# Two attention-style layers on one core: value products of two token chunks issued as one group, and more unit products in the first waits

## The chip, the cores and the metric

The kernel runs on one NeuronCore of a Trainium2 chip, in one launch. The metric is device time in microseconds (us) of a whole execution. The core has a tensor engine (TensorE, PE in the profile, its weight loads PEld), a vector engine (VectorE, DVE), a scalar engine (ScalarE, ACT), a general engine (GpSimd, POOL) and a queue engine that here only issues DMAs (SyncE, SP). Each engine works through its own instructions in order, and waits on semaphores for the others.

## The reference

Eight sequences of 512 tokens, 512 features, pass through two layers, all in float32. Layer 0 is linear attention with 8 heads; layer 1 is softmax attention with 16 heads of 32. Around each stands a layer norm, projections, a second norm with a scale and shift computed from a condition vector, a SiLU, an output projection and a residual. The change touches layer 1's middle:

```python
xn = layer_norm(x, norm_w, norm_b)
q = (xn @ q_w + q_b).reshape(Bx, Tx, H, -1)
k = (xn @ k_w + k_b).reshape(Bx, Tx, H, -1)
att = jnp.einsum('bnhl,bmhl->bnmh', q, k)
att = att + (1.0 - mask) * -1000000.0
att = jax.nn.softmax(att, axis=2)
v = ((xn @ v_w + v_b) * src_mask[:, :, None]).reshape(Bx, Tx, H, -1)
y = jnp.einsum('bnmh,bmhl->bnhl', att, v).reshape(Bx, Tx, Dx)
```

## The kernel before

**How it is recorded and ordered.** The body of the kernel does not issue instructions. It calls a recorder (`Order`), which keeps each operation with the tiles it reads and writes and an assumed cost. `place` then runs a list scheduler over the record twelve times, with priorities taken from the slack of the last round, and keeps the best; `issue` writes the instructions out in the order of the planned starts. So a change in what is recorded can move any instruction of any engine. Because `issue` writes nearly everything out, nearly every row of the profile has the line L501, and rows are told apart by tiles. `order.together(cost)` records several tensor-engine calls as one operation that is not split. `order.on("gpsimd", "vector")` lets the scheduler choose the engine.

**Buffers.** Tile pools are rings with a fixed number of buffers (`BUFS`, `BANKS`): ten 128x512 buffers named A, and eight PSUM banks named mm, which scores, maxima, projections, transposes, sums and value products share. PSUM banks may be taken out of the recorded order, A buffers may not.

**Layer 1.** The work goes by heads groups G = 4 b + g: sequence b, and four heads. For one G:
- `l1_qk` projects queries and keys, splits each into a high and a low part, and writes them to DRAM; `l1_stack` reads them back as stacked operands kst and qst of 98 and 106 rows, in rings of three (G % 3).
- `l1_max` makes 16 score products (98 rows, `mm<-kst,qst` in the profile), of which VectorE takes the row maxima (nm). They are transposed (`mm<-ident,mi`), copied to z and written by a 64 KB DMA into rows 98 to 106 of qst, so that the next products come out with the maximum subtracted.
- `l1_att` makes the 16 score products again, transposed (106 rows, `mm<-qst,kst`), one for each of four token chunks m and four heads j. ScalarE takes the exponential of each into an A buffer e.
- `l1_av` makes the four value products of chunk m: v's 32 columns of each head are the weights, e is streamed, and the four products lie side by side in the array's columns and write 32 rows each of one bank (`mm<-A,v`, 128*32). They accumulate over m. It also records the running sum acc = e(0) + e(1) + e(2) + e(3), four additions for each m > 0 on POOL or VectorE.
- `l1_den` sums acc over tokens by products with a constant eg, of the same 32-column form; it is recorded in one group with the value products of chunk 0 of the next G.

`l1_att` calls `l1_av(G, m - 1)` after the second score of chunk m, and chunk 3 is called at the beginning of the next G, so there are four groups of value products for each G. The last G has a form of its own (`l1_last`), in halves of 256 columns. Two exponentials, (m, j) = (2, 2) and (2, 3), go to the spare buffers bWq and bWk instead of A (`SPARE`), since the ten A buffers hold acc and the exponentials of two chunks. Around all this run the projections of the next sequence (`ahead`) and the second half of the one before (`behind_front`), fed in by small due times.

**Unit products.** `spare` (line 476) looks for planned idle time of TensorE. Before an operation that takes a fresh tile, it counts how many products of the identity with itself fit, at 240 ns each after a margin of 1000 ns, or 480 ns each for operations planned to start before 21 us (`WARM`). `issue` writes that many such products (line 497) into the bank that the operation is about to overwrite.

Of the kernel before, what the change touches and what calls it, by code (L numbers as in the profile page):

```python
# [21 lines left out]
P = 128  # L22
NC = S // P
# [164 lines left out]
class Room:  # L188
# [19 lines left out]
    def next(self):  # L208
        if self.free and self.head in self.queue:
            return self.queue.pop(self.head)  # L210
        if self.loose and len(self.free) > 1 and self.queue:
            return self.queue.pop(min(self.queue, key=lambda i: self.queue[i].key))


class Order:
# [260 lines left out]
    def spare(self):  # L476


        fill, last = {}, None
        for o in sorted((o for o in self.ops if o.engine == "PE"), key=lambda o: o.start):  # L480
            if o.fresh:
                since = max([last.start + last.takes["PE"][1] if last else IDENT] + [t.since for t in o.fresh])
                each = SPARE_TIME * (2 if o.start < WARM else 1)
                fill[o] = int(max(0.0, o.start - WEIGHTS - MARGIN - since) / each)
            last = o
        return fill

    def issue(self, nc, unit):
        fill = self.spare()
        for p in self.pools:  # L490
            p.build()
        with self.tc.manual_schedule():
            for o in sorted(self.ops, key=lambda o: (o.start, o.seq)):
                engine = getattr(nc, o.takes[o.engine][0])
                for _ in range(fill.get(o, 0)):
                    bank = o.fresh[0].root()
                    engine.matmul(bank[:, 0:P], unit[:, 0 : bank.shape[0]], unit, start=True, stop=True)
                for method, args, kw in o.calls:
                    args = [a.real() if isinstance(a, View) else a for a in args]
                    kw = {k: v.real() if isinstance(v, View) else v for k, v in kw.items()}  # L500
                    getattr(engine, method)(*args, **kw)  # L501
# [45 lines left out]
def kernel(ctx: ExitStack, tc: tile.TileContext, x, cond, mask0, mask1, w0, w1, out):  # L547
    real, order = tc.nc, Order(tc)
    nc = order
# [14 lines left out]
    def big(tag, name, dtype=F32, shape=(P, 512)):  # L564
        t = sb.tile(list(shape), dtype, name=name, tag=tag, bufs=BUFS[tag])
        if tag == "stk":
            nc.gpsimd.memset(t[:, :, 0:1].bitcast(F32), 0.0)
        return t

    def bank(tag, name, parts=P):  # L570
        tag = {"S": "mm", "ST": "mm", "a": "mm"}.get(tag, tag)
        return ps.tile([parts, 512], F32, name=name, tag=tag, bufs=BANKS[tag])

    def mm_bank(name):
        return bank("mm", name)

    def chunk(i):
        return slice(i * P, (i + 1) * P)
# [193 lines left out]
    st = {}  # L772
# [284 lines left out]
        st["max"] = G  # L1057
        yield

    SPARE = {(2, 2): "bWq", (2, 3): "bWk"}  # L1060

    def l1_att(G):
        b, g = divmod(G, 4)
        q, k = qst[G % 3], kst[G % 3]
        if g == 0:
            st["yT", b] = []
        assert st["max"] >= G
        st["yp", G] = bank("a", f"yT{G}")
        st["acc", G] = []
        for m in range(NC):  # L1070
            cur = []
            for j in range(4):
                sp = bank("ST", f"t{G}{m}{j}")
                nc.tensor.matmul(sp, k[:, j, chunk(m)], q[:, j, :], start=True, stop=True)
                e = big(SPARE.get((m, j), "A"), f"e{G}{m}{j}")
                nc.scalar.activation(e, sp, AF.Exp)
                cur.append(e)
                if j == 1 and m > 0:
                    l1_av(G, m - 1)
                yield  # L1080
            st["e", G, m] = cur

    def l1_av(G, m):
        b, g = divmod(G, 4)
        while len(st["L1", "v", b]) <= m:
            st["need"]()
        es, yp = st.pop(("e", G, m)), st["yp", G]
        with order.together(845.0 if m or not G else 1690.0):
            if m == 0 and G > 0:
                den = l1_den(G - 1)  # L1090
            for j in range(4):
                h = 4 * g + j
                nc.tensor.matmul(
                    yp[32 * j : 32 * j + 32, :],
                    st["L1", "v", b][m][:, 32 * h : 32 * h + 32],
                    es[j],
                    start=(m == 0),
                    stop=(m == NC - 1),
                )
        if m == 0 and G > 0:  # L1100
            l1_den_keep(G - 1, den)
        acc = st["acc", G]
        if m == 0:
            acc.extend(es)
        else:
            for j in range(4):
                with order.on("gpsimd", "vector"):
                    nc.gpsimd.tensor_tensor(acc[j], acc[j], es[j], ALU.add)
        if m == NC - 1:
            t = big("yT", f"yTs{G}")  # L1110
            nc.scalar.copy(t, st.pop(("yp", G)))
            st["yT", b].append(t)
# [58 lines left out]
    def l1_den(G):  # L1171
        g = G % 4
        den = mm_bank(f"den{G}")
        acc = st.pop(("acc", G))
        for j in range(4):
            nc.tensor.matmul(den[32 * j : 32 * j + 32, :], eg[:, g, :], acc[j], start=True, stop=True)
        return den

    def l1_den_keep(G, den):
        b, g = divmod(G, 4)  # L1180
        if g == 0:
            st["dn", b] = big("dn", f"dn{b}")
# [184 lines left out]
    def ahead(b):  # L1367

        n = b + 1
        if b > 0:  # L1370
            yield from values("L1", b)
            yield from l1_qk(4 * b + 3)
        if n < B:
            if b > 0:
                while st.get(("tail", b - 1)) != NC - 1:
                    yield 0
                load_x("L1", n, x1[n])
            yield from transpose_x("L1", n)
            for g in range(3 if n else 4):
                yield from l1_qk(4 * n + g)  # L1380
# [7 lines left out]
    for b in range(B):  # L1388
        plan = []
        if b > 0:  # L1390
            plan.append([behind_front(b), 6, 34 if b < B - 1 else 70, TAIL, 0.0])
            plan.append([ahead(b), 0, 20, HEAD, 0.0])
        if b < B - 1:
            plan.append([plan[1][0] if b else ahead(b), 34 if b else 0, 64, NEXT, 0.0])

        def step(p):
            c = next(p[0], None)
            if not c:
                return False
            p[4] += c  # L1400
            return True

        def pump(i):
            go = True
            while go:
                go = False
                for p in plan:
                    due = p[3] * min(1.0, max(0.0, (i + 1 - p[1]) / (p[2] - p[1])))
                    if p[4] < due and step(p):
                        go = True  # L1410

        def need():
            for p in reversed(plan):
                if step(p):
                    return
            raise AssertionError("nothing left")

        st["need"] = need
        for g in range(4):
            G = 4 * b + g  # L1420
            if G > 0:
                l1_av(G - 1, NC - 1)
            for i, _ in enumerate(l1_att(G) if G < NG - 1 else l1_last(G)):
                next(maxes, None)
                if b == B - 1 and g == 0 and i % 4 == 0:
                    for _ in range(2):
                        next(maxes, None)
                if i == STK and 0 < G < NG - 2:
                    while ("d", "Wq", G + 2) not in st:
                        need()  # L1430
                    l1_stack(G + 2)
                pump(16 * g + i)
        if b < B - 1:
            for p in plan:
                while step(p):
                    pass
    b = B - 1
# [50 lines left out]
```

## Time and profile before

| what | value |
|---|---|
| runs shown | 1376.63, 1385.99, 1386.61 us; median 1385.99 |
| profiled execution | 1377.14 us, of which the span from first to last instruction is 1375.1 |
| mean granted TensorE clock | 0.995 |
| score products, 98 rows (`mm<-kst,qst`) | 512, 201.6 us busy |
| score products, 106 rows, 512 wide (`mm<-qst,kst`) | 496, 185.4 us |
| value products from A buffers, 512 wide (`mm<-A,v`) | 868 records, 138.8 us |
| value products from bWq and bWk | 62 records each, 32.4 us each |
| sum products, 512 wide (`mm<-A,eg`) | 248 records, 33.0 us |
| unit products (L497) | 94 records, 13.4 us |
| additions of exponentials on POOL / VectorE (`A<-A,A`) | 249 at 1358 ns / 73 at 1176 ns |
| row maxima (VectorE, `nm<-mm`) | 512 at 683 ns |

Busy time counts records, which overlap: four products that lie side by side run together, and a product's end is modelled. So the distance from one start to the next says more about TensorE than the durations do. A product in float32 of the 32-column form leaves two records. The chain of work that ended last is read in order of time; a piece "PE mm x411" is a stretch in which TensorE waited for nothing.

### The profile page before, as it was taken

The page shows a single profiled execution, that of the slowest core. Times are in us where ns is not written, and L with a number is a line of the kernel's source. Part 1 is how long each engine was busy: PE and PEld are TensorE (multiplying, and loading weights), DVE is VectorE, ACT ScalarE, POOL GpSimd, SP SyncE. Part 2 cuts the span into 40 slices and gives each one's busy share as a digit, 9 for nine tenths or more (in the row PEclk, how much of TensorE's full clock was granted, in tenths as well). Part 3 has the DMA queues.
Part 4 walks back from the last instruction along what each step waited for, and adds up shares of the span by engine and source line. Part 5 has one row for each costly group of instructions (what it writes and reads, how often), then busy time and mean ns, then how long its engine had stood idle before and what let it go on. Part 6 is the DMA issues. An engine that isn't in the chain of part 4 may idle for free.

```text
span 1375.1 us, 21070 instructions
## 1 busy us (share of the span) xinstructions
PE 1351.2 (98%) x7457; PEld 951.9 (69%) x7457; DVE 1036.2 (75%) x1771; ACT 746.6 (54%) x1400; POOL 682.3 (50%) x748
## 2 busy tenths in 40 slices
PE   7999999999999999999999999999999999999998
PEld 6788788888888887556566566566566666656655
DVE  6676676667757778887878778778878867877886
ACT  4433334443344635646746855855864764774674
POOL 6222504133242625675556548538637645664673
PEclk8999999999999999999999999999999999999999
DMA  6332202022231374553264363462553545436222
GB/s 226 133 123 100 92 10 101 17 84 86 77 100 40 131 231 122 143 150 103 86 181 107 99 186 98 125 187 64 150 155 96 146 128 135 131 100 171 65 71 72
DMA packets 77376, 158.87 MB, mean 116 GB/s; under 512 B 8556, under 2 KB 8680, under 8 KB 77248
## 3 DMA queue, kind: packets, MB, share of 16 engines
q1 hardware_dynamic: 77152, 157.41, 39.0%
q8 instruction: 59, 0.97, 0.3%
q14 instruction: 45, 0.37, 0.1%
q0 software_dynamic: 64, 0.08, 0.0%
q10 hardware_dynamic: 56, 0.04, 0.0%
HBM read 104.92 MB, written 50.48 MB: 113 GB/s over the span
## 4 chain that ended last, share of the span: by engine, by line
PE 91%; DVE 3%; ACT 3%; DMA 2%; issue 1%; SPq 0%; ACTq 0%; POOL 0%; POOLq 0%
PE mm L501 91%; ACT mm L501 1%; DVE nm L501 1%; DMA qst<-z 1%; DVE A L501 1%; ACT y L501 1%; DMA kst<-dWk 0%; DVE xc L501 0%; ACT A L501 0%; DMA rawL0Wk<-in_L_cond_Wk 0%; DMA out<-y 0%; DMA v<-in_mask_BxS_ff 0%; DVE mi L501 0%; DMA rawL0Wv<-in_L_cond_Wv 0%; ACT hhL L501 0%
## 5 line engine op out<-in xcount | busy, mean ns | idle before, releaser
L501 POOL TENSOR_TENSOR A<-A,A 128x512 f32<-128x512 f32 x249 | 332.9, 1358 | 210.9 <-PE mm L501 144.4
L501 DVE TENSOR_REDUCE nm<-mm 128x1 f32<-128x512 f32 x512 | 332.4, 683 | 69.5 <-PE mm L501 66.3
L501 ACT ACTIVATE A<-mm 128x512 f32<-128x512 f32 x450 | 250.6, 602 | 142.2 <-PE mm L501 134.8
L501 PE MATMUL mm<-kst,qst 98*128 98x512 f32 x512 | 201.6, 420 | 2.2 <-DMA out<-y 1.7
L501 PE MATMUL mm<-qst,kst 106*128 106x512 f32 (+1 forms) x528 | 192.3, 404 | 2.2 <-DMA qst<-z 1.3
L501 PEld LDWEIGHTS mm<-kst,qst 98*128 98x128 f32 x512 | 96.1, 191 | 71.8 <-issue 19.3
L501 PE MATMUL mm<-A,v 128*32 128x512 f32 (+1 forms) x932 | 143.8, 587 | 0.0
L501 PEld LDWEIGHTS mm<-qst,kst 106*128 106x128 f32 x528 | 97.3, 189 | 53.1 <-issue 14.2
L501 POOL TENSOR_TENSOR y<-y,bo 128x512 f32<-128x512 f32 x60 | 78.4, 1312 | 100.9 <-DMA y<-in_x 98.3
L501 PE MATMUL mm<-Wvh,xT 128*128 128x512 f32 x384 | 120.5, 403 | 0.0
L501 PE MATMUL mm<-xT,Wkh 128*128 128x512 f32 x384 | 117.7, 414 | 1.1 <-ACT xT L501 0.8
L501 ACT ACTIVATE mm<-mm,cols 128x512 f32<-128x512 f32 x64 | 48.2, 752 | 122.7 <-PE mm L501 122.7
L501 POOL TENSOR_SCALAR v<-bWv,cols 128x512 f32<-128x512 f32 x64 | 47.4, 753 | 114.6 <-PE mm L501 114.6
L501 ACT ACTIVATE y<-mm,shL,scL 128x128 f32<-128x128 f32 (+1 forms) x144 | 76.3, 530 | 51.1 <-PE mm L501 48.5
L501 PE MATMUL mm<-ident,xc 128*128 128x128 f32 x512 | 91.6, 282 | 10.1 <-DVE xc L501 7.2
L501 DVE TENSOR_TENSOR A<-A,A 128x512 f32<-128x512 f32 x73 | 85.2, 1176 | 13.6 <-PE mm L501 11.1
L501 PEld LDWEIGHTS mm<-ident,xc 128*128 128x128 f32 x512 | 64.4, 143 | 39.1 <-DVE xc L501 8.6
L501 PEld LDWEIGHTS mm<-xT,Wkh 128*128 128x128 f32 x384 | 70.0, 192 | 22.4 <-ACT xT L501 6.0
L501 PEld LDWEIGHTS mm<-Wvh,xT 128*128 128x128 f32 x384 | 71.9, 190 | 16.5 <-issue 1.7
L501 ACT ACTIVATE mm<-mm,shL,scL 128x128 f32<-128x128 f32 (+2 forms) x152 | 76.0, 500 | 7.2 <-PE mm L501 7.2
L501 PE MATMUL mm<-xT,Wqh 128*128 128x512 f32 x256 | 76.5, 399 | 0.3 <-DVE nm L501 0.2
L501 POOL MEMSET bWk<- 64x4 f32 (+1 forms) x24 | 5.8, 243 | 136.2 <-PE mm L501 135.4
(206 smaller groups left out, 2724.0 us busy)
## 6 DMA issues: line engine op xcount, KB each, us to landing
kst<-dWk SPq DMA_DIRECT2D x96, 256.0 KB
qst<-dWq SPq DMA_DIRECT2D x96, 256.0 KB
dWk<-hl SPq DMA_DIRECT2D x32, 512.0 KB
dWq<-hl SPq DMA_DIRECT2D x32, 512.0 KB
xc<-in_x SPq DMA_DIRECT2D x32, 256.0 KB
y<-in_x SPq DMA_DIRECT2D x32, 256.0 KB
x<-y SPq DMA_DIRECT2D x32, 256.0 KB
xc<-x SPq DMA_DIRECT2D x32, 256.0 KB
```

The lines of the kernel that those rows point to most:

```text
L501: getattr(engine, method)(*args, **kw)
```

## The change

Three things, all in recording and ordering; the arithmetic is the same.

1. `l1_av` takes a tuple of chunks. `l1_att` calls it for chunk 0 after the second score of chunk 1, and for chunks 1 and 2 together after the second score of chunk 3; chunk 3 follows at the beginning of the next G, as before. The eight value products of chunks 1 and 2 are one operation that isn't split. The value bank yp is taken from the ring when the first value products are recorded, not at the start of `l1_att`.
2. The two exponentials that use the spare buffers are those of chunk 1 (j = 2, 3), not of chunk 2.
3. Unit products are counted before any tensor operation that is a transpose or opens an accumulation, not only before one that takes a fresh tile. For operations planned before 21 us they are counted at 300 ns each after a margin of 300 ns. They are no wider than the tile that is about to be written.

```diff
-            if o.fresh:
+            method, args, kw = o.calls[0]
+            if method == "transpose" or kw["start"]:
+                each, margin = (300.0, 300.0) if o.start < WARM else (SPARE_TIME, MARGIN)
                 since = max([last.start + last.takes["PE"][1] if last else IDENT] + [t.since for t in o.fresh])
-                each = SPARE_TIME * (2 if o.start < WARM else 1)
-                fill[o] = int(max(0.0, o.start - WEIGHTS - MARGIN - since) / each)
+                fill[o] = int(max(0.0, o.start - WEIGHTS - margin - since) / each)
...
-                    bank = o.fresh[0].root()
-                    engine.matmul(bank[:, 0:P], unit[:, 0 : bank.shape[0]], unit, start=True, stop=True)
+                    to = o.calls[0][1][0].real()
+                    n = min(P, to.shape[1])
+                    engine.matmul(to[:, 0:n], unit[:, 0 : to.shape[0]], unit[:, 0:n], start=True, stop=True)
...
-    SPARE = {(2, 2): "bWq", (2, 3): "bWk"}
+    SPARE = {(1, 2): "bWq", (1, 3): "bWk"}
...
-        st["yp", G] = bank("a", f"yT{G}")
...
-                if j == 1 and m > 0:
-                    l1_av(G, m - 1)
+                if j == 1 and m in (1, 3):
+                    l1_av(G, (0,) if m == 1 else (1, 2))
...
-    def l1_av(G, m):
+    def l1_av(G, ms):
...
-        es, yp = st.pop(("e", G, m)), st["yp", G]
-        with order.together(845.0 if m or not G else 1690.0):
-            if m == 0 and G > 0:
-                den = l1_den(G - 1)
-            for j in range(4):
...
+        ess = [st.pop(("e", G, m)) for m in ms]
+        den = ms[0] == 0 and G > 0
+        with order.together(845.0 * (len(ms) + den)):
+            if den:
+                dp = l1_den(G - 1)
+            if ms[0] == 0:
+                st["yp", G] = bank("a", f"yT{G}")
+            yp = st["yp", G]
+            for m, es in zip(ms, ess):
+                for j in range(4):
...
-                l1_av(G - 1, NC - 1)
+                l1_av(G - 1, (3,))
```

More of the change, by code (lines that the diff above doesn't have):

```diff
@@ L1077, in l1_att @@
                 cur.append(e)
-                if j == 1 and m > 0:
-                    l1_av(G, m - 1)
+                if j == 1 and m in (1, 3):
+                    l1_av(G, (0,) if m == 1 else (1, 2))
                 yield
             st["e", G, m] = cur
-    def l1_av(G, m):
+    def l1_av(G, ms):
         b, g = divmod(G, 4)
-        while len(st["L1", "v", b]) <= m:
+        while len(st["L1", "v", b]) <= ms[-1]:
             st["need"]()
-        es, yp = st.pop(("e", G, m)), st["yp", G]
-        with order.together(845.0 if m or not G else 1690.0):
-            if m == 0 and G > 0:
-                den = l1_den(G - 1)
-            for j in range(4):
[L1092 to L1101, printed above, removed]
+        ess = [st.pop(("e", G, m)) for m in ms]
[8 more added lines that the diff above has]
+                for j in range(4):
+                    h = 4 * g + j
+                    nc.tensor.matmul(
+                        yp[32 * j : 32 * j + 32, :],
+                        st["L1", "v", b][m][:, 32 * h : 32 * h + 32],
+                        es[j],
+                        start=(m == 0),
+                        stop=(m == NC - 1),
+                    )
+        if den:
+            l1_den_keep(G - 1, dp)
         acc = st["acc", G]
-        if m == 0:
-            acc.extend(es)
-        else:
+        for es in ess:
+            if not acc:
+                acc.extend(es)
+                continue
             for j in range(4):
@@ L1108, in l1_av @@
                     nc.gpsimd.tensor_tensor(acc[j], acc[j], es[j], ALU.add)
-        if m == NC - 1:
+        if ms[-1] == NC - 1:
             t = big("yT", f"yTs{G}")
```

## The prediction, made before the changed kernel had run

> **What bounds the kernel now.** I read the page's busy and slice rows first, then the chain in order of time, the busy time by stage, and the TensorE timeline around the groups that the change touches.
>
> ```profile
> PE 1351.2 (98%) x7457; PEld 951.9 (69%) x7457; DVE 1036.2 (75%) x1771; ACT 746.6 (54%) x1400; POOL 682.3 (50%) x748
> PEclk8999999999999999999999999999999999999999
> PE 91%; DVE 3%; ACT 3%; DMA 2%; issue 1%; SPq 0%; ACTq 0%; POOL 0%; POOLq 0%
> ...
> 883.00:992.00 109.00, 108.31 (x551) 68.45 (x549) 85.54 (x137) 69.86 (x136) 65.13 (x62) 1.00 0.48 131
> 992.00:1101.00 109.00, 107.84 (x548) 68.37 (x549) 85.26 (x137) 69.43 (x135) 65.05 (x61) 1.00 0.47 130
> ...
> 897.86 80.33 PE mm L501 x411
> 980.46 7.36 PE mm L501 x32
> 988.45 3.72 DMA qst<-z
> 992.31 14.24 PE mm L501 x76
> ```
>
> TensorE is busy for 98% of the span and carries 91% of the chain. The windows' columns are stretch, length, busy us (count) of TensorE, its weight loads, VectorE, ScalarE and POOL, granted clock, DMA share, GB/s. In the second layer a batch takes 108.7 us (the chain's 992.31 returns at 1101.03), of which TensorE fills 108; VectorE, the next, has 85. So time can come only out of TensorE's own stream: useless intervals inside it, or waits. One wait stands on the chain in every batch, for the 64 KB write of the row maxima into the stacked operand (DMA qst<-z).
>
> The inside of the stream is seen in the timeline of TensorE (start, duration, what; one product of the 32-column kind leaves two records, so x8 is a group of four):
>
> ```profile
> 813.83 1.10 PE L501 MATMUL mm<-xT,Wql 128*128 128x512 f32 x4
> 814.86 1.06 PE L501 MATMUL mm<-A,eg 128*32 128x512 f32 x8
> 815.74 1.04 PE L501 MATMUL mm<-A,v 128*32 128x512 f32 x8
> 816.71 0.50 PE L501 MATMUL mm<-kst,qst 98*128 98x512 f32 x1
> 817.04 0.40 PE L501 MATMUL mm<-qst,kst 106*128 106x512 f32 x1
> ...
> 819.38 0.39 PE L501 MATMUL mm<-qst,kst 106*128 106x512 f32 x1
> 819.70 1.07 PE L501 MATMUL mm<-A,v 128*32 128x512 f32 x8
> 820.70 0.50 PE L501 MATMUL mm<-kst,qst 98*128 98x512 f32 x1
> 821.04 0.39 PE L501 MATMUL mm<-qst,kst 106*128 106x512 f32 x1
> ```
>
> Starts count here, since ends are modelled. Full-width products start 0.235 us apart. A lone group: from the last full start before it (819.38) to the second after it (821.04) is 1.66; less two full intervals (0.47), a group costs 1.19. A double group (sums `eg`, then values): from 813.83 + 1.10 - 0.39 = 814.54 to 817.04 is 2.50, less 0.47 is 2.03. So a group that joins another costs 0.84 to 0.86 instead of 1.19: entering and leaving the 32-column form costs 0.34. Over all groups between full-width products the medians are 1.661 (76 lone ones) and 2.517 (20 double ones): 2 x 1.661 - 2.517 - 0.466 = 0.339.
>
> **The merge.** The change issues token chunks 1 and 2 as one group. In the order that the built programs issue there are 143 unbroken runs of 32-column products before and 111 after: 31 heads groups have one run of eight value products in place of two of four, and one lone group of sums joins values. The 528 value and 132 sum products stay the same in number, and the scheduler did not break the pairs up. 32 x 0.339 = **-10.8 us**, all of it in a stream with nothing else to wait for. That two value groups in a row cost no more than sums and values in a row isn't seen in this trace (none stand together); the nearest row is the emb products of layer one, which accumulate twice into one bank with pass starts 0.41 to 0.43 us apart, as in the double group. Bounds: -8 to -11.5.
>
> **What the merge moves.** Chunk 1's exponentials wait until chunk 2's are there, so two of them move to the spare buffers bWq and bWk, which chunk 2 had. Ten A buffers and two spares are then all held (4 running sums, 8 exponentials). In the issue order a score whose exponential reuses a buffer comes within 1.5 us of the group that frees it 49 times, against 17 of 496. TensorE does not wait for the exponential itself, but for the PSUM bank behind it. Banks are taken again at the same least distance, about 1.2 us of TensorE work (48 times after, 31 before); before, those 31 waited 0.12 us in all. I take nothing for it, with 0 to 3 us as bounds. In return the value bank is taken at the first group, not at the first score, which leaves the ring of eight a bank more for some 4 us in each heads group.
>
> Seven additions of exponentials go from POOL (306 to 299) to VectorE (78 to 85): 7 x 1.176 us (the A<-A,A row) is 8 us of VectorE over some 840, in batches where it has 24 of 109 free. No price. The DMAs on SP are the same in number and nearly in order; POOL's queue issues none there.
>
> **The maxima's wait.** The work standing between the transposes of the maxima and the first score that needs them back is 4.2 us in the worst heads group of a batch, counted from the issue order by the intervals above, where the wait is 0.55 to 0.62; in the changed order it is 4.7. Six such waits, 0.70, 0.37, 0.24, 0.59, 0.56 and 0.62, sum to 3.1 us; a half us more cover leaves about 1. **-2 us**, bounds -3 and +1.
>
> **The first waits.** The unit products (an identity times itself) grow from 8, 4 and 0 before the first three starts to 15 (twelve columns wide), 9 and 3. Rows:
>
> ```profile
> 5.70:9.10 3.40, 1.29 (x10) 1.07 (x9) 1.87 (x6) 2.65 (x4) 2.97 (x4) 1.00 0.86 295
> 9.10:22.80 13.70, 9.12 (x28) 6.54 (x29) 8.37 (x10) 7.39 (x13) 5.60 (x8) 0.50 0.98 326
> 22.80:30.00 7.20, 7.20 (x33) 5.94 (x32) 6.78 (x10) 3.98 (x8) 7.20 (x6) 1.00 0.38 138
> ...
> 12.27 1.11 PE L501 MATMUL mm<-ident,xc 128*128 128x128 f32 x4 [5.28 <-DVE xc L501]
> ...
> 18.33 2.07 PE L501 MATMUL mm<-xT,Wkh 128*128 128x512 f32 x4 [0.82 <-ACT xT L501]
> ```
>
> TensorE is full at 5.7, has 1.29 us of work in the next 3.4, and runs at half clock from 9.1 to 22.8. Between 18.33 and 22.79 that costs: at 0.427 a product about 10.4 are done. At 0.233 ScalarE bounds, which gives a transposed chunk every 1.27 us (18.28 to 22.08), each good for five: 18 would be done, 7.6 x 0.233 = -1.8 us. If the clock rises only in the next 3.4 us step (19.4), -1.3.
>
> Here the Trainium skill speaks on both sides. "TensorE: Matmul & The Clock Gate", section "What's actually happening", has the clock rise after one busy window of some 3.4 us; the trace agrees in the step (5.72, 9.13, 22.79 are multiples of 3.41 apart), and by it more filling gives the -1.3 to -1.8. Its section "PE-mode transpose" says that transposes do not count as busy in the same way. The row fits that too: 12.55 to 15.96 holds some 2.8 us of transposes and stays cold. By this rule the window that ends at 19.4 still has 1.4 us of transposes, the clock stays down, and the three unit products before the first projection run at half speed: 17.5 + 3 x 0.43 = 18.8 against the 18.33 at which its operand is there, +0.5. I take **-1.0**, nearer to the filled windows. Overrun of the earlier ones: 15 narrow ones at no more than the wide ones' 0.47 end by 9.1, 9 more at half clock by 13.1, 0.8 late at the worst; the constants that the narrow ones delay are first read at 16.9. Bounds -2 to +1.
>
> The tail fillers (23 before, 16 after) stand in waits that real work or latency ends: nothing.
>
> **Sum.** -10.8 - 2 - 1.0 + 0.3 for small new waits = -13.5 us. The profiled execution took 1377.14 (span 1375.1), which gives 1363.6. But it stands at the low end of the runs shown, 1376.63, 1385.99 and 1386.61; at their median level the same sum is 1385.99 - 13.5 = 1372.5. What makes the 9.5 us between these levels, no row shows, so both are kept in the range.
>
> **Rivals.**
> - The gain is only the merge's, or less: the start stays cold, the maxima's wait returns in another group. -8 to -10.8, so 1375 to 1378. For it: these two terms rest on covers counted from an order, not seen. 30%.
> - The value products find no neighbour's price: if a second value group in a row drained like a first, 31 x 0.339 falls away and -3 is left, 1383. Against it: sums and values in a row don't. 5%.
> - Slower, by buffers: at chunk 3 the ring of twelve exponentials is full, the next four wait for the merged group and then for POOL's addition (1.36) before ScalarE's 0.60 and the score banks behind. If TensorE runs out of other work for one addition in each of 31 heads groups, that is 31 x 1.36 = +42, 1414; it decides from 13.5 / 31 = 0.44 us in each. For it: 49 tight reuses instead of 17. Against: some 80 us of a batch's chain are unbroken TensorE work, and bank distances hold. 8%.
> - The change does not do what it says (pairs split by the scheduler): excluded by the order, 31 runs of eight.
>
> **How the numbers follow.** The forecast has 57%. One per cent, 13.9 us, is about what a measurement here tells from no change, and the forecast lies just under it: its sum reaches it in two cases of five, and runs at the lower level would pass it (1364 is 1.6% under the median shown). Together faster 0.46, within 1% 0.46, slower 0.08. The range runs from the low level with the larger bounds (1361) to the small-gain cases at the upper level (1381).
>
> **What would show it.** In the changed profile: runs of x16 records `mm<-A,v` whose second half starts 0.86 to 0.88 after the first, the batch at 107 us, the DMA qst<-z piece shorter or gone, the half-clock row ending before 22.8, VectorE near 86 a batch. Wrong if the batch stays at 108.7, if waits of TensorE for ScalarE's A appear at chunk 3, or if the second half starts 1.2 after the first.

## The result, and the profile after

The changed kernel takes 1389.85 us (median of 20 runs, 1381.19 to 1392.51), the kernel before 1386.3 beside it (20 runs, 1376.2 to 1389.15): ratio 1.0049, 95% interval 1.0031 to 1.0068. The forecast was 1372.5 with a range of 1361 to 1381, so it was wrong in sign and outside its range. One thing is needed to read the ratios below: runs of the kernel before fall into two groups, about 1375 to 1383 and 1384 to 1390 us, in shares that differ from one set of runs to the next, and its median moves between them.

The profiled execution has a span of 1388.1 us, against 1375.1. These are lines of its page: busy time by engine, the granted clock in 40 slices, the chain's shares, and the additions of exponentials.

```profile
PE 1352.8 (97%) x7473; PEld 963.7 (69%) x7473; DVE 1055.5 (76%) x1778; ACT 742.6 (54%) x1400; POOL 676.6 (49%) x741
...
PEclk9999999999999999999999999999999999999999
...
PE 90%; DVE 5%; ACT 4%; POOL 1%; issue 1%; DMA 0%; ACTq 0%; POOLq 0%; DVEq 0%
...
L503 POOL TENSOR_TENSOR A<-A,A 128x512 f32<-128x512 f32 x245 | 335.7, 1391 | 186.3 <-PE mm L503 134.4
...
L503 DVE TENSOR_TENSOR A<-A,A 128x512 f32<-128x512 f32 x77 | 96.3, 1253 | 16.3 <-PE mm L503 10.3
```

TensorE's modelled busy time has not fallen, though 32 changes of form were saved, and the DMA share of the chain is gone (2% before). VectorE and ScalarE have taken shares. The mean granted clock is 0.987 (0.995 before): the slices are too coarse to show it, since a stretch at half clock here lasts 3.41 us, a tenth of a slice.

Dividing the span at the first 98-row product of each sequence (the starts of every 64th `mm<-kst,qst`) shows where the 13.0 us are, in us:

| from the trace | before | after | after - before |
|---|---|---|---|
| start to the first maxima | 502.9 | 500.7 | -2.2 |
| sequence 0 | 80.2 | 78.5 | -1.6 |
| sequence 1 | 115.9 | 120.5 | +4.6 |
| sequences 2 to 6, together | 543.9 | 544.6 | +0.7 |
| the last, to the end | 132.3 | 143.8 | +11.5 |

Forecast were about -1.7 in each sequence. Sequences 0 and 1 are read together, +3.0: one group of value products (8 records `mm<-A,v`, 72 against 64 in sequence 0) moved over the line between them. So there are three things to explain: nothing gained in the middle, 3.0 lost at the start of layer 1, and 11.5 at the end. The trace of the kernel before is one of its lower group, and the last row is mostly the distance between the groups: an unmerged kernel below has 142.4 there.

**The middle.** The chain of waits (start, duration, what) no longer has the DMA qst<-z piece in a batch. In its place it runs through ScalarE:

```profile
17.84 74.25 PE mm L503 x449
...
895.91 81.59 PE mm L503 x422
977.52 0.46 ACT y L503
...
981.53 0.51 ACT bWk L503
982.04 0.97 ACT A L503 x2
983.02 0.48 ACT h L503
983.54 17.78 PE mm L503 x88
```

TensorE's timeline at that place, with what it waited for in brackets:

```profile
980.87 0.51 PE L503 MATMUL mm<-qst,kst 106*128 106x512 f32 x1
982.10 0.98 PE L503 MATMUL mm<-qst,kst 106*128 106x512 f32 x2 [0.72 <-ACT bWk L503]
983.54 1.48 PE L503 MATMUL mm<-Woh,h 128*128 128x512 f32 x4 [0.47 <-ACT h L503]
984.82 1.91 PE L503 MATMUL mm<-Wol,h 128*128 128x512 f32 x4
...
988.45 0.40 PE L503 MATMUL mm<-kst,qst 98*128 98x512 f32 x1
988.78 0.62 PE L503 MATMUL mm<-A,v 128*32 128x512 f32 x2
...
989.66 1.04 PE L503 MATMUL mm<-A,v 128*32 128x512 f32 x8
990.63 0.50 PE L503 MATMUL mm<-kst,qst 98*128 98x512 f32 x1
990.97 0.40 PE L503 MATMUL mm<-qst,kst 106*128 106x512 f32 x1
```

and its windows there (stretch, length, busy us (count) of TensorE, weight loads, VectorE, ScalarE, POOL, granted clock, DMA share, GB/s):

```profile
977.40:980.87 3.47, 2.97 (x15) 1.73 (x14) 3.42 (x6) 2.46 (x7) 3.15 (x3) 1.00 0.47 171
980.87:984.28 3.41, 2.23 (x7) 1.20 (x7) 2.59 (x5) 3.41 (x8) 2.16 (x2) 1.00 1.01 248
984.28:987.69 3.41, 3.41 (x12) 2.28 (x11) 2.93 (x4) 1.65 (x5) 3.41 (x4) 0.50 0.50 149
987.69:991.10 3.41, 3.41 (x24) 1.48 (x23) 2.38 (x4) 2.53 (x6) 1.56 (x2) 1.00 0.27 57
```

A burst of eight small ScalarE activations (y<-mm and mm<-mm,shL,scL) delays the exponential of chunk 1 to 981.5. TensorE starts 7 products in a window of 3.41 us, is busy for 2.23 of it (0.65), and has half its clock for the next 3.41 us. This repeats in four of the five middle batches, which take 109.2 us each. The other one, sequence 2, has the same two waits but not the lost clock, and takes 107.68. So the half clock costs some 1.5 us of a batch, and the bare waits less. There the second wait falls into the next window, and the first window keeps 2.63 us of work (0.77), as these lines of the timeline and the windows show:

```profile
765.22 0.98 PE L503 MATMUL mm<-qst,kst 106*128 106x512 f32 x2 [0.73 <-ACT bWk L503]
766.66 1.20 PE L503 MATMUL mm<-Woh,h 128*128 128x512 f32 x4 [0.47 <-ACT h L503]
...
762.41:765.83 3.42, 2.63 (x11) 1.29 (x9) 2.67 (x5) 3.35 (x9) 1.83 (x2) 1.00 0.81 218
765.83:769.24 3.41, 2.94 (x15) 2.06 (x15) 3.29 (x5) 3.21 (x8) 3.41 (x4) 1.00 0.97 248
```

The kernel before has the same burst, and a lone value group lies in it. Its timeline:

```profile
982.13 0.51 PE L501 MATMUL mm<-kst,qst 98*128 98x512 f32 x1
982.57 1.93 PE L501 MATMUL mm<-A,v 128*32 128x512 f32 x8
984.43 0.50 PE L501 MATMUL mm<-qst,kst 106*128 106x512 f32 x1
```

It is the group of chunk 1, which the change has moved behind the second score of chunk 3: here 988.78 to 989.66, right behind the half-clock stretch. In the burst it lasts 1.93 us, not the usual 1.07. From the last full product before it to the second after it are 2.63 us in each of the five middle batches, 0.97 more than the 1.66 of a lone group. So TensorE lost about 1 us to the burst in the kernel before too, but inside a group that it counts as busy, with the clock full.

**The end.** These are the VectorE, POOL and TensorE lines near 1260 us, from the timelines:

```profile
1258.10 7.04 DVE L503 CAST mi<-nm 128x16 fp32r<-128x16 f32 x1
...
1257.69 1.29 POOL L503 TENSOR_TENSOR A<-A,bWk 128x512 f32<-128x512 f32 x1
1258.93 6.17 POOL L503 TENSOR_TENSOR A<-A,A 128x512 f32<-128x512 f32 x5
...
1265.40 1.01 PE L503 MATMUL mm<-ident,mi 128*8 128x128 f32 x4 [4.30 <-DVE mi L503]
```

A cast of a 128x16 tile, 0.40 us in the median of the five around this place, begins while POOL is adding and lasts until POOL's run of additions ends (1265.10). TensorE waits 4.30 us and then has half clock in two windows. The Trainium skill has the rule: "SBUF — State Buffer", section "SBUF: two separate sides", says that VectorE in a fast mode, or with two operands in SBUF, and GpSimd take one port pair for a whole instruction, the loser blocked. No row names the port. The trace goes further than the page: the cast was held through six additions in a row, each an instruction of its own. It is not held so every time; another trace below has it through after one.

**The start of layer 1.** A VectorE addition ends just behind a run of POOL's in the same way, and the maxima behind it are late (timelines of POOL, VectorE and TensorE):

```profile
580.32 8.72 POOL L503 TENSOR_TENSOR A<-A,A 128x512 f32<-128x512 f32 x7
...
585.84 3.76 DVE L503 TENSOR_TENSOR A<-A,A 128x512 f32<-128x512 f32 x1
...
590.25 0.50 PE L503 MATMUL mm<-kst,qst 98*128 98x512 f32 x1 [1.55 <-DVE nm L503]
591.45 0.56 PE L503 MATMUL mm<-kst,qst 98*128 98x512 f32 x1 [0.69 <-DVE nm L503]
```

A half-clock window follows here as well. VectorE instructions longer than 2.5 us number 3 in this trace (this addition, the cast at 1258.10 and a cast of 3.79 us at 542.55), none in that of the kernel before. The merge frees two chunks of exponentials at once, so eight additions fall due together, and POOL's rows of ten or more additions number 8 against 2 (pauses under 0.2 us let pass). But rows of ten or more POOL instructions of any kind number 21 in both, so that longer runs are what catches VectorE is not shown.

### The profile page after: what moved, and what is told of

It reads as the page before. It is cut to its first block, busy times and chain, and to the rows that moved or that the text cites. A ratio compares the mean times of both kernels' runs of the same rounds, so it can differ in the third digit from the quotient of the medians.

```text
span 1388.1 us, 21133 instructions
## 1 busy us (share of the span) xinstructions
PE 1352.8 (97%) x7473; PEld 963.7 (69%) x7473; DVE 1055.5 (76%) x1778; ACT 742.6 (54%) x1400; POOL 676.6 (49%) x741
## 4 chain that ended last, share of the span: by engine, by line
PE 90%; DVE 5%; ACT 4%; POOL 1%; issue 1%; DMA 0%; ACTq 0%; POOLq 0%; DVEq 0%
PE mm L503 89%; DVE nm L503 1%; ACT mm L503 1%; DVE A L503 1%; ACT y L503 1%; DVE mi L503 1%; DVE xc L503 1%; ACT A L503 0%; ACT xT L503 0%; DVE xT L503 0%; POOL A L503 0%; ACT h L503 0%; PE mm L499 0%; ACT bWk L503 0%; DMA v<-in_mask_BxS_ff 0%
## 5 line engine op out<-in xcount | busy, mean ns | idle before, releaser
L503 PE MATMUL mm<-qst,kst 106*128 106x512 f32 (+1 forms) x528 | 198.9, 411 | 5.5 <-ACT bWk L503 4.5
L503 PE MATMUL mm<-A,v 128*32 128x512 f32 (+1 forms) x932 | 132.3, 588 | 0.9 <-ACT A L503 0.9
L503 DVE TENSOR_TENSOR A<-A,A 128x512 f32<-128x512 f32 x77 | 96.3, 1253 | 16.3 <-PE mm L503 10.3
L503 PE MATMUL mm<-ident,xc 128*128 128x128 f32 x512 | 86.0, 278 | 6.4 <-DVE xc L503 3.6
L503 PE MATMUL mm<-Woh,h 128*128 128x512 f32 x224 | 71.5, 422 | 5.3 <-ACT h L503 5.3
```

## The experiments

Each edit is against the kernel that its first words name. Unless said otherwise the ratio is to the kernel before, with its 95% interval. In the versions that merge only some heads groups, the first-waits code is that of the changed kernel.

**The two halves of the change.** First the kernel before again, as a measure of what can be told:

> The kernel before, unchanged, once more, for the granted clock of each of its runs (only one profiled clock is known: 0.995 at 1377 us). Theory A (half-clock windows make the levels): runs near 1386 show a mean clock near 0.988, runs near 1377 near 0.995; 9.5 us lost at half clock are 19 us of half clock, 0.0069 of the mean. Theory B (the levels come from DMAs or other waits): the clock is 0.995 in all runs, whatever their time. Ratio to before 1.000 under both.

1385.43, ratio 1.0002 (0.9982 to 1.0022). Neither theory fits: of the twelve runs at 1385 and more, ten show a clock of 0.990 to 0.993, not 0.988, and two show 0.995 and 0.996, as the shortest runs do. So half clock alone does not make the upper group. The trace, of a run at 1377.38, had the end at 131.9 us, like the first trace of this kernel.

Then the kernel before with the new counting of unit products alone (part 3 of the change):

> Only the unit products of the change (15, 9 and 3 in the first waits); value products in four groups as before. Theory A: the half-clock stretch from 9.1 to 22.8 us is gone, TensorE is some 2.1 us ahead from there on (17.84 to 92.11 in the changed kernel against 18.33 to 94.26 before), no other half-clock window than before has; 1375 where before has 1377, ratio 0.997 to 0.999. Theory B (waits alone): the same -2. Rival C (early filling itself draws later half-clock windows): the clock falls below 0.99 and the ratio is above 1.003.

1383.78, ratio 0.9985 (0.9960 to 1.0011), which by itself tells nothing from no change; but its trace reaches the first maxima at 500.6 us instead of 502.9. And the changed kernel with the old counting, so the merge alone:

> Only the merge of chunks 1 and 2 and the moved spare buffers; unit products as before. Theory A: the profile has the half-clock window once a batch as the whole change has (875, 984, 1093, 1202 us), the mean clock is about 0.982 (the changed kernel's 0.987 less the start's 0.005), 1391 to 1392, ratio 1.005 to 1.007. Rival C: without the early filling no such windows; batch 107.5 us, ratio 0.992.

1393.56, ratio 1.0082 (1.0050 to 1.0115). The merge is what costs; the first waits bring something. The trace of the version with the first waits alone gave a find. Its instructions near 1260 us are those of the kernel before, in the same order, but the cast has another fate. First its VectorE and POOL timelines, then that of the kernel before:

```profile
1256.51 8.38 DVE L503 CAST mi<-nm 128x16 fp32r<-128x16 f32 x1
...
1256.24 1.28 POOL L503 TENSOR_TENSOR A<-A,A 128x512 f32<-128x512 f32 x1
...
1259.95 4.91 POOL L503 TENSOR_TENSOR A<-A,A 128x512 f32<-128x512 f32 x4
```

```profile
1259.36 1.04 DVE L501 CAST mi<-nm 128x16 fp32r<-128x16 f32 x1
...
1259.09 1.28 POOL L501 TENSOR_TENSOR A<-A,A 128x512 f32<-128x512 f32 x1
1260.33 1.30 POOL L501 TENSOR_TENSOR A<-A,bWq 128x512 f32<-128x512 f32 x1
```

Where the cast slips in between two additions (1260.33), the end takes 132.3 us; where it waits for the whole run (to 1264.86), 142.4. That 10 us is about the distance between the two groups of times. In both traces the cast begins 0.27 us after an addition does, so its place within the addition does not decide.

**Feeding the clock.** The changed kernel with 115 more unit products, placed in the waits of layer 1 that its trace showed (by the number of tensor calls issued so far):

```diff
+                    if calls in self.FEED:
+                        i = pe.index(o)
...
+                            n = self.FEED[calls]
```

> The changed kernel with 115 more unit products (0.11 us each record, two records) put into the second layer's waits that its profile shows, 12 of them in each batch, 8 of these in the 5 us before the half-clock window. They write into a PSUM bank that is free and about to be overwritten; the waits themselves stay. Theory A (half-clock windows, not the waits, eat the gain): the windows at 875, 984, 1093, 1202 are gone, the batch goes from 109.2 to 107.5 us, mean clock 0.997 or more, 1373 to 1378, ratio to before 0.989 to 0.995. Theory B (the waits of the merged order cost the time, the clock only follows): time stays at 1386 to 1392, ratio 1.003 or more, since no wait is taken away and up to 5 us of filling may be added.

1380.1, ratio 0.9975 (0.9956 to 0.9994), clock 1.0 in all runs, no half-clock stretch before the last microsecond, batch 108.07 instead of 109.2. The clock's part is shown, though neither the time (1373 to 1378) nor the batch (107.5) of theory A was reached: the waits themselves stay, now filled. The filling costs something too, since sequence 2 of the changed kernel, with full clock and no such filling, takes 107.68.

**Moving the cast.** ScalarE makes the cast instead of VectorE, in the changed kernel, in the kernel before, and in the fed one (there without the 21 unit products that stood in the waits for the cast):

```diff
+                if o.calls[0][0] == "tensor_copy" and o.calls[0][1][0].tile.tag == "mi":
+                    engine, o.calls = nc.scalar, [("copy", *o.calls[0][1:])]
```

> The whole change, order unchanged, but the 32 small casts mi<-nm (128x16) go from VectorE to ScalarE at the same place of the order. In the changed kernel's profile one of them, at 1258 us, lasts 7.04 us and ends when POOL's row of five additions ends; TensorE waits 4.3 us for it and the clock falls. Theory P (the cast, SBUF to SBUF on VectorE, waits for a port that POOL's additions hold): no cast longer than 1.5 us, no half-clock window at 1264, 5 to 8 us less than the changed kernel: 1382 to 1385, ratio to before 0.997 to 0.999. Theory Q (7 us is only what the place in the order costs; the subtraction behind it waits as long): less than 2 us gained, ratio 1.003 or more. The windows at 875, 984, 1093, 1202 stay under both.

> The kernel before with the same casts on ScalarE. Theory P: its upper level (1385 to 1389, 60% of the runs) is the same cast caught behind POOL's additions at about 1260 us, so that level is gone, all runs lie within 1373 to 1382, median ratio about 0.994. Theory Q: two levels as before, ratio 1.000.

> The changed kernel with the unit products in its waits (without the 18 and 3 that stood in the two waits for the cast) and the casts on ScalarE. Theories A and P together: full clock throughout as in the fed kernel (1380.1), and the 7.05 us cast at 1252 gone: 1372 to 1375, ratio to before 0.990 to 0.992, faster than before's lowest run (1376.2). If A held but not P: 1378 to 1381.

1385.19, ratio 1.0014 (0.9997 to 1.0031); 1384.34, ratio 0.9983 (0.9962 to 1.0004); 1382.47, ratio 0.9993 (0.9976 to 1.0009). The wait was not removed but handed on: the subtraction behind the cast, also on VectorE, lasted 6.82, 7.73 and 6.82 us in the three. The first of them:

```profile
1256.30 6.82 DVE L505 TENSOR_TENSOR mi<-nm,mi 128x16 fp32r<-128x16 f32 x1 [0.27 <-ACT mi L505]
```

The kernel before kept its two groups, as theory Q had it, and the trace with 7.73 us is one of its upper group (1387.67). The first time lies between the two theories; its trace gains in sequence 1 (118.9 instead of 120.5), not at the end (143.0). All this told that the place matters, not the operation.

**Which merge uncovers the burst.** The burst falls into heads group 1 of each sequence. In the changed kernel, that group alone keeps chunks 1 and 2 apart, with the old spare buffers:

```diff
-                if j == 1 and m in (1, 3):
+                if g == 1 and j == 1 and m > 0:
+                    l1_av(G, (m - 1,))
+                elif g != 1 and j == 1 and m in (1, 3):
...
```

> The change, but in the second heads group of each batch (g = 1), where the half-clock window starts, chunks 1 and 2 are issued apart again, with the old spare buffers. 23 merges in place of 31, 119 runs of 32-column products. Theory A with the cover as its cause (a lone group of value products used to fill TensorE while ScalarE works through eight small activations): the two waits of 0.92 and 0.73 us at that place shrink to 0.45 as before, no half-clock window there, batch 107.9 us (108.72 less 3 x 0.34 less the wait for the maxima), ratio 0.992 to 0.998. Theory D (any new order has its own clusters of waits; the group's cover is not what matters): windows at half clock once a batch at another place or the same, ratio 1.002 to 1.008.

1372.48, ratio 0.9917 (0.9889 to 0.9945): with 23 of 31 merges it beats both kernels. Against the lower group alone the gain is less, some 4 us: its runs begin at 1371.75, those of the kernel before beside it at 1375.69. The value group stands in the burst again (timeline of TensorE), no batch has a half-clock stretch, and no cast of 7 us occurs:

```profile
979.26 0.50 PE L503 MATMUL mm<-qst,kst 106*128 106x512 f32 x1
979.69 1.66 PE L503 MATMUL mm<-A,v 128*32 128x512 f32 x8
981.28 0.50 PE L503 MATMUL mm<-qst,kst 106*128 106x512 f32 x1
```

As controls, heads group 3 alone kept apart, and heads group 1 alone merged (the same diff with 3 for 1, and with the conditions exchanged):

> The changed kernel, but heads group 3 of each sequence (instead of heads group 1, as in the run before) keeps chunks 1 and 2 as two groups, with the old spare buffers there; 24 merged pairs remain, 118 runs of 32-column products. Theory of the cover (what is lost is the lone group that bridged ScalarE's burst of eight small activations, and that burst falls into heads group 1): the waits before chunk 1's scores of heads group 1 stay, a half-clock stretch of 3.41 us stands in each of four or five batches, the batch takes 109.2 us, the time is 1386 to 1391, ratio 1.000 to 1.004. Rival (any heads group left apart gives the buffers or the schedule enough air): as with heads group 1 apart, 1371 to 1376, ratio 0.990 to 0.993, no half-clock stretch per batch.

> The other way round: only heads group 1 of each sequence has chunks 1 and 2 merged (8 pairs), the other three keep two groups and the old spare buffers. Theory of the cover: nearly the whole loss with a quarter of the saving: half-clock stretches in each of four or five batches, batch about 109.5 to 110, time 1386 to 1394, ratio 1.000 to 1.006. Rival (loss in proportion to the merges made): less loss than with 31 merges, at most 1384, ratio below 0.999, no half-clock stretch per batch.

1380.47, ratio 0.9975 (0.9954 to 0.9995), and 1374.52, ratio 0.9956 (0.9937 to 0.9976). Both miss what I wrote down for the theory of the cover, and in the second the rival came out (at most 1384, no half-clock stretch in a batch). Half of the theory holds: wherever heads group 1 is merged, the wait for chunk 1's exponential is there. Here in the run with only that group merged:

```profile
981.41 0.49 PE L503 MATMUL mm<-qst,kst 106*128 106x512 f32 x1 [0.79 <-ACT bWk L503]
```

It is 0.85 with heads group 3 apart, 0.72 in the changed kernel, and absent with heads group 1 apart. But a wait of 0.8 us is not yet a lost clock. In both controls four transposes and not the h products follow it, and the window's busy share comes to about 0.77 with only heads group 1 merged (never a drop in a batch) and 0.70 to 0.74 with group 3 apart (a drop in one batch of five). In the changed kernel it is 0.65, and it drops each time. So a second wait in the same window decides, as between sequence 2 of the changed kernel and its other batches. Where that falls depends on the order and on where the windows cut it. The second control's batch of 107.7 us gains more than one merge gives. The group with 0.97 us of hidden wait is gone from its burst, but a bare wait of 0.79 us has come, so not all of that gain is explained. The low time of this control is also due to its end (133.9 us), without the cast's wait.

Unit products in the two half-clock places that the version with heads group 1 apart still has (20 of them):

> The version with heads group 1 apart, plus 20 unit products in three waits of layer 1's first maxima and of the last sequence, where its own profile has its two half-clock stretches (591.6 and 1328.8 us). Theory that the clock follows TensorE's share of work in a 3.41 us window: both stretches go, 2 x 1.7 us less, 1368 to 1371, ratio 0.987 to 0.990. Rival (the unit products overrun the waits and delay the chain by what the clock gives back): 1371 to 1375, ratio 0.990 to 0.993.

1372.83, ratio 0.9928 (0.9908 to 0.9949): the two stretches went, another came at 1350.7, and the time is the same as without. The rival is nearer.

**Breaking POOL's run.** One instruction is added. POOL copies the finished tile of heads group 28 to a scratch tile before its next addition, so it must stop until the cast and subtraction are through:

```diff
+                if self.paced and o.engine == "POOL":
+                    nc.gpsimd.tensor_copy(pace, self.paced.real())
+                    self.paced = None
...
```

> The changed kernel with one instruction more: before its first addition of exponentials that is planned behind the maxima of heads group 28 (mi28), POOL copies that 128x16 tile into a scratch tile, so that it must wait for VectorE's cast and subtraction there instead of running on. Theory P (the 7.04 us cast at 1258 us is VectorE waiting through POOL's unbroken run of additions, and the half-clock stretch behind it follows from it): the cast takes about 1 us, from 1258 on 8 to 10 us less, the part from heads group 28's first maxima to the end falls from 143.8 to 134 to 136 us, the time is 1379 to 1382, ratio 0.995 to 0.998. Rival Q (the wait moves to the next VectorE operation with two inputs or to POOL's additions, as it did when ScalarE took the cast): 1387 to 1391, ratio 1.001 to 1.005.

1383.48, ratio 1.0043 (1.0030 to 1.0056). In the timelines the cast takes 0.90 us and POOL waits 0.31:

```profile
1260.24 0.90 DVE L512 CAST mi<-nm 128x16 fp32r<-128x16 f32 x1
...
1261.42 0.20 POOL L504 CAST pace<-mi 128x16 fp32r<-128x16 f32 x1 [0.31 <-DVE mi L512]
```

The end falls from 143.8 to 136.1, so the cast's wait and the clock behind it cost 7.7 us there. The time is 1.5 us above the range that I gave: all five middle batches had the half-clock stretch here, one more than in the trace that I counted from. The ratio missed its own range because the kernel before was at 1378 in the runs beside it.

> The kernel before with the same one instruction. Theory P (the two levels of the kernel before, 1376 to 1381 and 1384 to 1389, are executions in which this cast slips in between two additions and executions in which it waits for the whole run): the upper level goes, nearly all runs at 1376 to 1381, median 1376.5 to 1379, ratio 0.992 to 0.996. Rival Q: two levels stay, median 1384 to 1387, ratio 0.998 to 1.002.

1379.31, ratio 1.0009 (1.0002 to 1.0016). All runs lie in the lower group, but so did those of the kernel before here (1375.03 to 1380.27). So this run decides nothing about the two groups.

> The changed kernel with 115 unit products in layer 1's waits (no half-clock stretches) and the one POOL instruction. Theory P and the clock theory together (what the changed kernel loses against its forecast is the half clock of each batch and the cast's wait): 1371 to 1376, ratio 0.990 to 0.994, near the forecast of 1372.5. Rival (the cast's wait was already covered by the unit products put there, so taking it away gives nothing more): 1379 to 1381, ratio 0.996 to 0.999.

1379.58, ratio 1.0015 (1.0007 to 1.0022): nothing gained over feeding alone. But 18 of the unit products had been put into the very wait that was now gone. Without them:

> As the run before (unit products in layer 1's waits, and the one POOL instruction), without the 18 unit products that stood in the wait behind the 7 us cast, since that wait is gone. Theory (the run before gained nothing because these 18 products, about 0.24 us each, stood in TensorE's stream with nothing left to wait for): 4 us less, 1374.5 to 1377, no half-clock stretch before 1370. Rival (the cast's wait is covered in any case by the chain behind it): 1379 to 1381 as before.

1375.99, ratio 0.9971 (0.9959 to 0.9982), as expected: 3.6 us less. One half-clock stretch that was not expected stands at 15.69 us. And the changed kernel once more, beside the same runs of the kernel before:

> The changed kernel once more, beside the runs of the kernel before on the same chip. If the kernel before has its lower level alone there (1375 to 1381, as beside the last three runs) and the cast's wait is what makes the levels, the changed kernel has some runs at 1380 to 1384 too, and otherwise 1388 to 1392. If the levels belong to the chip and not to the cast, it is at one level with the kernel before.

1390.09, ratio 1.0060 (1.0040 to 1.0080), 1385.69 to 1392.53, while 23 of the 32 runs of the kernel before were below 1381.2. Neither expectation came: the changed kernel has no run at 1380 to 1384 there and is not level with the kernel before. Its trace has the cast at 7.04 us again.

## Why the prediction was wrong

Its pieces, with what they measured:

- **The merge, -10.8: right in itself.** From the last full product before the merged group (988.45) to the second after it (990.97) are 2.52 us, as 2 x 1.661 - 0.466 - 0.339 = 2.517 had it; the second half starts 0.88 after the first. The 23 merged groups that stand between full-width products have a median of 2.523. A second value group costs no more than sums did; that rival falls.
- **The maxima's wait, -2: right in kind.** The DMA qst<-z piece has left the chain of the batches, where it made TensorE wait 0.39 to 0.45 us in three of them; the 2 us as a sum were not measured apart.
- **The first waits, -1.0: the right sign, too small.** The long piece begins at 17.84 instead of 18.33 and ends 2.2 us earlier (92.09 against 94.26). The rule of the section "PE-mode transpose", cited in the prediction, held me back from the larger value, and the trace speaks against it as far as keeping the clock goes. The first of these windows (columns as above) holds some 0.8 us of unit products, up to 12.3, and then transposes alone, the next begins with nine more transposes, and the clock stays full:

```profile
11.50:14.90 3.40, 2.08 (x15) 1.41 (x14) 3.40 (x3) 0.00 (x0) 3.40 (x3) 1.00 0.92 310
14.90:22.80 7.90, 7.06 (x35) 5.24 (x36) 4.38 (x9) 6.25 (x11) 0.64 (x2) 1.00 0.97 329
```

With the unit products alone the first window would be busy for 0.24 of its time, and every window below 0.48 in these traces lost the clock. In the last fed version the same window begins later, holds 0.36 us of unit products (0.51 with the transposes), and lost it (the stretch at 15.69).

- **The step that failed: "What the merge moves", put at nothing with 0 to 3 us, and the "+0.3 for small new waits".** I counted how much TensorE work lies between two uses of a bank, 1.2 us at least, and took it for enough. It was not where ScalarE is late: a score product needs nothing of an exponential but its bank, and the one at 982.10 waits 0.72 us for ACT bWk, behind eight small activations. I did not ask what the lone group of chunk 1 had been covering. It was TensorE's work during that burst, at 982.57 in the kernel before, between a product for the maxima and a score. The burst makes TensorE wait hardly longer than before: 1.2 us bare, instead of 0.97 hidden in the group. But the bare wait also costs the clock, some 1.5 us in four of five batches: they take 109.2 us instead of 107, and the one where the clock held takes 107.68.
- **"Seven additions ... No price" failed too.** I counted VectorE's hours, where the price lay in a cast and an addition of VectorE caught behind POOL's additions: 7.7 us for the cast, by the version that breaks the run. The seven additions that move are not shown to be what catches them, and the cast is caught in an unmerged version too. What differs is how often: of the 32 runs of the changed kernel shown, one is below 1384.
- **The slower rival had the wrong place.** It looked for the wait at chunk 3 and for POOL's addition in each of 31 heads groups. The wait came at chunk 1, in one heads group of four, for ScalarE.

By medians, some 17 us lie between forecast (1372.5) and result (1389.85), and the forecast began at the upper group. If the upper group is the caught cast, so that 142.4 is the end to compare with, an estimate from the parts of the traces is: 9.6 for the five batches (544.6 against 5 x 107), 6.3 for sequences 0 and 1 (199.0 against 192.7), some 2 for the end, less 1.1 at the start.

From the profiled spans, whose trace before is of the lower group: 1388.1 less 5.6 with POOL's run broken (1382.5), less 7.5 with the clock fed as well (1375.0), leaves 13.4 to the forecast's 1361.6 (1363.6 less the 2.0 around the span). Of these, some 5 are the five batches at 108.07 instead of 107, where the waits remain, only filled; some 5 are sequences 0 and 1 (198.1 against 192.7); most of the rest is the end (135.0). The addition caught at the start of layer 1 is only about 1 of these 5. In the first fed version, with the same order there, it takes 1.27 us instead of 3.75, and sequence 1 takes 118.7 instead of 119.6. For the start of layer 1 and the end the runs show where the time is, not all of what makes it.

Still open is what makes the two groups of times of the kernel before. The two traces at 1.04 and 8.38 us for the same cast fit the distance, and so does the upper-group trace with the cast on ScalarE, where the subtraction takes 7.73. But every trace of the unchanged kernel before is of the lower group, so it was not seen in the kernel itself. Why the changed kernel falls to the long wait nearly always was not tried either; its cast stands ready at 1258.10, inside an addition, as in both of the others.

## What to carry to other kernels

Before joining two pieces of work, look at what the piece that moves lies beside in the timeline: a lone group that costs a third of a microsecond too much may be the only thing that keeps the engine busy through another engine's burst. Saving work on the bounding engine pays only while its waits stay spread out, so join pieces where the neighbours have work, and leave one out where they don't, as in the version with three of four. Price an addition handed between VectorE and POOL by what its run blocks, not by the free time of the engine.

## What the hardware did that was not expected

- The clock does not need a whole idle window to fall. In the batches of layer 1, windows of 3.41 us in which TensorE is busy for a share of 0.65 lost half the clock for the next one in all 23 cases of five traces, those of 0.70 to 0.74 in one of five. Of all windows at 0.76 and more, one did (0.79). The modelled share is not the whole rule: outside these batches windows from 0.49 on kept the clock at times, as in the kernel before:

```profile
1309.61:1313.02 3.41, 1.66 (x9) 0.23 (x3) 2.02 (x4) 2.56 (x5) 2.59 (x8) 1.00 0.79 189
1313.02:1316.44 3.42, 3.42 (x15) 2.71 (x16) 2.97 (x5) 2.29 (x4) 1.33 (x2) 1.00 0.28 77
```

The Trainium skill's page "TensorE: Matmul & The Clock Gate", section "Why this matters for your kernels", warns of idle gaps over about 3 us; here 0.7 and 0.5 us in one window were enough.
- The windows lie on a fixed grid, and the batch fell into step with it: where the stretch stands in each of them, batches take 109.13 to 109.25 us, and 32 windows of 3.413 are 109.2.
- Moving a blocked VectorE operation to another engine did not free the chain, since the next one was blocked for 6.8 us in its place; a 0.20 us copy that made POOL pause for 0.31 us did (0.90 us for the cast).
